# One load of 128 rows, split into a transfer of 80 rows and one of 48 rows in four pieces

## The chip, the cores and the metric

The kernel runs on one core of a Trainium2 chip. The metric is the device time of one execution in microseconds (us), the median of several runs. Profiles come from one execution taken with the hardware profiler on. The core has a matrix engine (PE), a vector engine (DVE), a scalar engine (ACT), GpSimd (POOL) and a sync engine (SP), each with an instruction queue of its own, and 16 DMA engines that carry what the queues issue.

## The reference

`x` is 128 samples of 128 channels by 1024 times in float32 (512 KB a sample, 64 MB in all). Each sample has a subject number from 0 to 7, and there are eight 128 x 128 weight matrices. Every sample gets its subject's matrix applied to its channels, and the result is added to the sample:

```python
w = weights[subjects]                      # (128, 128, 128)
out = jnp.einsum('bct,bcd->bdt', x, w)
return x + out
```

64 MB are read and 64 MB written, whatever the order.

## The kernel before

Four samples (`G * H`, with `G = 2` and `H = 2`) make a slot's content; there are 32 such groups (`NT`), called i, and 12 slots in SBUF (`xs`), so group i uses slot i % 12. Half a group, two samples, is a pair; pairs are the steps of the computation (64 of them, called j). A sample's number within its group is q.

All work is in one critical section whose order is written out by hand. Each engine runs its own list and meets the others at semaphores.

- ACT only issues loads. The first (L161) brings all eight weight matrices into `w_all`. Then come 128 loads, one a sample, through `load` (L121) and `transfer` (L50). A load reads the sample's 128 rows of 4 KB as 32 pieces of 16 KB (four consecutive rows each, `ROWS = 4`) and writes 128 partitions of 4 KB. From group 12 on ACT waits (L167) until the store of the group that held the slot before has landed.
- POOL copies, for each sample, the matrix of its subject out of `w_all` into one of four buffers `ws` (L196). The first copy of a pair waits for the pair's two loads (L200, semaphore `s_pair`), the second follows and signals `s_copied` (L201).
- PE multiplies (L206): two matmuls of 512 columns a sample, four a pair, into one of two PSUM buffers `ps`.
- DVE adds the products to the samples in place (L217), one addition a pair.
- SP issues the stores (`store`, L130), one of 2 MB for a whole group after its second pair; the first and the last group go in smaller stores. The last sample's store (L231) ends the program, together with ACT's waits for the stores of the last 12 groups (L228 to L230).

A transfer adds 16 to its semaphore once all of it has landed. The load of the pair's two samples therefore brings `s_pair` to 32 above what the slot's earlier use left (`loaded`, L116; `emptied`, L111).

Of the kernel before, what the change touches and what calls it, by code (L numbers as in the profile page):

```python
# [30 lines left out]
G = 2  # L31
H = 2
# [3 lines left out]
SLOTS = 12  # L36
# [5 lines left out]
DMA = 16  # L42

IDLE = 3

ROWS = 4
QUEUES = {mybir.EngineType.SP: "qSPDynamicHW", mybir.EngineType.Activation: "qActDynamicHW"}


def transfer(nc, engine, out, in_):  # L50

    later, nc._always_lower_symbolic_ap = nc._always_lower_symbolic_ap, False
    ins, outs = engine.lower_ap_dma(in_), engine.lower_ap_dma(out)
    nc._always_lower_symbolic_ap = later
    return engine.add_instruction(  # L57
        mybir.InstDMACopy(
            name=nc.get_next_instruction_name(),
            engine=engine.engine,  # L60
            ins=ins,
            outs=outs,
            mode="Copy",
            cce_op=ALU.bypass,
            queue=QUEUES[engine.engine],
        )
    )


@with_exitstack  # L70
def kernel(
    ctx: ExitStack,
    tc: tile.TileContext,
    x: bass.AP,
    subjects: bass.AP,
    weights: bass.AP,
    out: bass.AP,
):
    nc = tc.nc
    B, C, T = x.shape  # L80
    S, _, D = weights.shape
    NT = B // (G * H)

    def sbuf(name, *shape, dtype=F32):
        return ctx.enter_context(nc.sbuf_tensor(name, list(shape), dtype)).ap()

    given, near, wrap, index = (
        sbuf(name, 1, B, dtype=I32) for name in ("given", "near", "wrap", "index")
    )
    w_all = sbuf("w_all", C, S, D)  # L90
    ws = [sbuf(f"w{i}", C, 1, D) for i in range(W_SLOTS)]
    zeros = sbuf("zeros", C, N)
    xs = [sbuf(f"x{i}", C, H * G, T) for i in range(SLOTS)]
    ps = [
        ctx.enter_context(nc.psum_tensor(f"ps{i}", [D, G, T], F32)).ap() for i in range(P_SLOTS)
    ]

    s_given = tc.alloc_semaphore("s_given")
    s_wall = tc.alloc_semaphore("s_wall")
    s_index = tc.alloc_semaphore("s_index")  # L100
    s_zeros = tc.alloc_semaphore("s_zeros")
    s_copied = tc.alloc_semaphore("s_copied")
    s_product = tc.alloc_semaphore("s_product")
    s_added = tc.alloc_semaphore("s_added")

    s_pair = [[tc.alloc_semaphore(f"s_pair{i}_{h}") for h in range(H)] for i in range(SLOTS)]


    s_first = tc.alloc_semaphore("s_first")

    def emptied(i, h):  # L111

        turns = i // SLOTS
        return (DMA * G + (DMA if h == H - 1 else 0)) * turns

    def loaded(i, q):  # L116

        h = q // G
        return s_pair[i % SLOTS][h], emptied(i, h) + DMA * G

    def load(engine, i, q):  # L121
        k, h = i % SLOTS, q // G
        transfer(
            nc,
            engine,
            xs[k][:, q, :],
            x[i * H * G + q].rearrange("(a r) t -> a (r t)", r=ROWS),
        ).then_inc(s_pair[k][h], DMA)

    def store(i, q0, q1):  # L130
        k, b = i % SLOTS, i * H * G
        transfer(
            nc,
            nc.sync,
            out[b + q0 : b + q1].rearrange("g d t -> d g t"),
            xs[k][:, q0:q1, :].rearrange("d (o g) t -> d o (g t)", g=min(G, q1 - q0)),
        ).then_inc(s_first if i == 0 and q1 == G else s_pair[k][(q1 - 1) // G], DMA)

    with tc.tile_critical():  # L139

        nc.sync.dma_start(given, subjects.rearrange("(o b) -> o b", o=1)).then_inc(s_given, DMA)

        nc.vector.memset(zeros, 0.0).then_inc(s_zeros, 1)  # L143
        nc.tensor.wait_ge(s_zeros, 1)
        for _ in range(IDLE):
            nc.tensor.matmul(  # L146
                ps[P_SLOTS - 1][:, G - 1, :N], zeros[:, :D], zeros, start=True, stop=True
            )

        nc.vector.wait_ge(s_given, DMA)
        nc.vector.tensor_scalar(near, given, -S, S - 1, ALU.max, ALU.min).then_inc(s_index, 1)  # L153
        nc.vector.wait_ge(s_index, 1)
        nc.vector.tensor_scalar(wrap, near, 0, S, ALU.is_lt, ALU.mult).then_inc(s_index, 1)  # L155
        nc.vector.wait_ge(s_index, 2)
        nc.vector.tensor_tensor(index, near, wrap, ALU.add).then_inc(s_index, 1)  # L157
        nc.gpsimd.wait_ge(s_index, 3)


        nc.scalar.dma_start(w_all, weights.rearrange("s c d -> c s d")).then_inc(s_wall, DMA)  # L161
        for i in range(NT):
            k = i % SLOTS
            if i == SLOTS:
                nc.scalar.wait_ge(s_first, DMA)
            if i >= SLOTS:
                nc.scalar.wait_ge(s_pair[k][H - 1], emptied(i, H - 1))  # L167
            for q in range(H * G):
                load(nc.scalar, i, q)


        for j in range(NT * H):
            i, q0, q1 = j // H, j % H * G, (j % H + 1) * G
            k = i % SLOTS
            p = ps[j % P_SLOTS]

            ahead = j < P_SLOTS
            if ahead:  # L180
                nc.tensor.wait_ge(*loaded(i, q0))
            for q in range(q0, q1):
                b = i * H * G + q
                if b % R == 0:
                    _, subject = nc.values_load_multi_w_load_instructions(
                        index[0:1, b : b + R],
                        engines=[mybir.EngineType.Pool],
                        min_val=0,
                        max_val=S - 1,
                        skip_runtime_bounds_check_because="the index is clamped on the chip above",  # L190
                    )
                if b == 0:
                    nc.gpsimd.wait_ge(s_wall, DMA)
                if not ahead and q == q0:
                    nc.gpsimd.wait_ge(s_added, j - P_SLOTS + 1)
                copy = nc.gpsimd.tensor_copy(  # L196
                    ws[b % W_SLOTS], w_all[:, bass.ds(subject[b % R], 1), :]
                )
                if not ahead and q == q0:
                    copy.wait_op(*loaded(i, q0), "sem-ge")  # L200
            copy.then_inc(s_copied, 1)  # L201

            nc.tensor.wait_ge(s_copied, j + 1)
            for q in range(q0, q1):
                for t in range(0, T, N):
                    mm = nc.tensor.matmul(  # L206
                        p[:, q % G, t : t + N],
                        ws[(i * H * G + q) % W_SLOTS][:, 0, :],
                        xs[k][:, q, t : t + N],
                        start=True,  # L210
                        stop=True,
                    )
            mm.then_inc(s_product, 1)

            mine = xs[k][:, q0:q1, :]
            nc.vector.wait_ge(s_product, j + 1)
            nc.vector.tensor_tensor(  # L217
                mine, p, mine, ALU.add
            ).then_inc(s_added, 1)

            if i == 0 or q1 == H * G or i == NT - 1:
                nc.sync.wait_ge(s_added, j + 1)
                store(i, q0 if i in (0, NT - 1) else 0, q1 - (b == B - 1))

    with tc.tile_critical() as waits:
        for i in range(NT - SLOTS, NT):  # L228
            nc.scalar.wait_ge(s_pair[i % SLOTS][H - 1], emptied(i + SLOTS, H - 1))
        nc.scalar.wait_ge(s_pair[(NT - 1) % SLOTS][0], emptied(NT - 1 + SLOTS, 0) + DMA)  # L230
    last = nc.sync.dma_start(out[B - 1], xs[(NT - 1) % SLOTS][:, H * G - 1, :])  # L231

    tc.add_manual_dep(
        last.ins,
        waits.name,
        mybir.DependencyInfo(mybir.DependencyClass.NoSync, mybir.DependencyReason.SCHED_ONLY),
        reason="the end of the program waits for it",
    )
# [27 lines left out]
```

## Time and profile before

| What | Value |
|---|---|
| time, median of 3 runs | 325.85 us (325.69 to 325.96) |
| time of the profiled run | 326.15 us |
| its span, first to last instruction | 324.4 us |
| PE busy | 240.2 us (74%) |
| DVE busy | 147.9 us (46%) |
| POOL busy | 34.3 us (11%) |
| HBM read, written | 67.63 MB, 67.11 MB |
| issue of a load on ACT's queue, shortest, median, longest | 478, 1255, 4269 ns |
| SP's last wait, for the stores | 18.8 us |

The span is what the trace shows of the program; the run's time has 1.75 us more around it. An engine's busy share is a mean over the whole span and says nothing of who waits for whom; that is read from the idle time before a group of instructions and from what ended it. DMA figures are means over the 16 DMA engines. The page has the load queue as q10 (issued by ACT), the store queue as q1 (issued by SP) and instruction packets, with which the engines' programs are brought in, as q8 and q14.

### The profile page before, as it was taken

To read this page: it belongs to the slowest core of one execution; us is meant where nothing else is said; L and a number is where in the kernel's file an instruction comes from. 1 tells how busy PE (TensorE), PEld (TensorE's weight loads), DVE (VectorE), ACT (ScalarE), POOL (GpSimd) and SP (SyncE) were. 2 spreads that over 40 slices of the span, in tenths; PEclk is the share of its full clock that TensorE was granted. 3 is DMA by queue.
4 is the path that set the end of the run, shared out by engine and by line. 5 is a ranking of instruction groups with operands and counts; after the bars stand their busy time and mean duration, and the time that the engine had idled before them with its cause. 6 is when DMAs were issued, how large, how long until landed. Compare 5 with 4: busy or idle time off the path is not lost.

```text
span 324.4 us, 1608 instructions
## 1 busy us (share of the span) xinstructions
PE 240.2 (74%) x518; PEld 94.5 (29%) x518; DVE 147.9 (46%) x68; POOL 34.3 (11%) x132
## 2 busy tenths in 40 slices
PE   7999987888888888888988888888888768000000
PEld 2444432333333333333333333333333323000000
DVE  1475754555555555555555555554554553200000
POOL 1011110111111111111011111111111010000000
PEclk9999999999999999999999999999999999855555
DMA  7999999999999999999999999999999999999995
GB/s 263 402 418 426 426 421 425 425 425 423 428 425 422 427 418 427 427 424 424 428 423 421 423 427 426 419 429 426 423 426 427 417 435 417 425 427 424 429 426 243
DMA packets 16074, 134.85 MB, mean 416 GB/s; under 512 B 2625, under 2 KB 3650, under 8 KB 3906
## 3 DMA queue, kind: packets, MB, share of 16 engines
q10 hardware_dynamic: 7184, 67.64, 49.8%
q1 hardware_dynamic: 8882, 67.11, 49.3%
q8 instruction: 4, 0.07, 0.1%
q14 instruction: 4, 0.03, 0.0%
HBM read 67.63 MB, written 67.11 MB: 415 GB/s over the span
## 4 chain that ended last, share of the span: by engine, by line
PE 41%; DVE 20%; issue 18%; POOL 4%; DMA 2%; POOLq 1%; ACTq 0%; SPq 0%
PE ps L206 41%; DVE x L217 20%; POOL w L196 4%; DMA x<-in_x_dram 2%; POOLq L196 1%; ACTq L57 0%; ACTq L161 0%; ACTq L262 0%; SPq L139 0%
## 5 line engine op out<-in xcount | busy, mean ns | idle before, releaser
L206 PE MATMUL ps<-x,w 128*128 128x512 f32 x512 | 234.7, 604 | 33.6 <-POOL w L196 32.9
L217 DVE TENSOR_TENSOR x<-ps,x 128x2048 f32<-128x2048 f32 x64 | 146.7, 2292 | 128.1 <-PE ps L206 128.1
L206 PEld LDWEIGHTS ps<-x,w 128*128 128x128 f32 x512 | 92.6, 189 | 176.5 <-issue 92.3
L196 POOL COPY w<-w_all 128x128 f32 x128 | 34.1, 296 | 237.2 <-DMA x<-in_x_dram 207.2
L146 PE MATMUL ps<-zeros 128*128 128x512 f32 x6 | 5.5, 1088 | 1.7 <-DVE zeros L143 1.7
L146 PEld LDWEIGHTS ps<-zeros 128*128 128x128 f32 x6 | 1.8, 328 | 3.7 <-issue 2.1
L143 DVE MEMSET zeros<- 128x512 f32 x1 | 0.5, 485 | 1.1 <-SPq L139 1.1
L153 DVE TENSOR_SCALAR near<-given 1x128 int32<-1x128 int32 x1 | 0.2, 216 | 0.6 <-DMA given<-in_itok_B_dram 0.6
L157 DVE CUSTOM_DVE_ANT_0 index<-near,wrap 1x256 uint16<-1x256 uint16 x1 | 0.3, 278 | 0.0
L155 DVE TENSOR_SCALAR wrap<-near 1x128 int32<-1x128 int32 x1 | 0.2, 215 | 0.0
L253 POOL MEMSET const-float32-0.0<- 128x1 f32 x1 | 0.1, 99 | 0.2 <-issue 0.2
L253 POOL MEMSET const-bfloat16-1.0<- 128x1 bf16 x1 | 0.1, 102 | 0.0
L253 POOL MEMSET const-uint8-127<- 128x1 uint8 x1 | 0.1, 102 | 0.0
L253 POOL MEMSET const-float32-1.0<- 128x1 f32 x1 | 0.1, 99 | 0.0
## 6 DMA issues: line engine op xcount, KB each, us to landing
x<-in_x_dram ACTq DMA_DIRECT2D x128, 512.0 KB, 32.2
out_dram<-x SPq DMA_DIRECT2D x30, 2048.0 KB, 46.9
out_dram<-x SPq DMA_DIRECT2D x3, 1024.0 KB, 13.8
out_dram<-x SPq DMA_DIRECT2D x2, 512.0 KB, 21.0
w_all<-in_L_cond_weights_dram ACTq DMA_DIRECT2D x1, 512.0 KB, 4.3
given<-in_itok_B_dram SPq DMA_DIRECT2D x1, 0.5 KB
```

The source lines that it names most:

```text
L143: nc.vector.memset(zeros, 0.0).then_inc(s_zeros, 1)
L146: nc.tensor.matmul(ps[P_SLOTS - 1][:, G - 1, :N], zeros[:, :D], zeros, start=True, stop=True)
L153: nc.vector.tensor_scalar(near, given, -S, S - 1, ALU.max, ALU.min).then_inc(s_index, 1)
L155: nc.vector.tensor_scalar(wrap, near, 0, S, ALU.is_lt, ALU.mult).then_inc(s_index, 1)
L157: nc.vector.tensor_tensor(index, near, wrap, ALU.add).then_inc(s_index, 1)
L196: copy = nc.gpsimd.tensor_copy(ws[b % W_SLOTS], w_all[:, bass.ds(subject[b % R], 1), :])
L206: mm = nc.tensor.matmul(p[:, q % G, t : t + N], ws[(i * H * G + q) % W_SLOTS][:, 0, :], xs[k][:, q, t : t + N], start=True, stop=True,)
L217: nc.vector.tensor_tensor(mine, p, mine, ALU.add).then_inc(s_added, 1)
L253: nc = _bacc.Bacc("TRN2", target_bir_lowering=False, num_devices=1)
```

## The change

The load of sample q = 1 of group i = 8 (in slot 8, the 34th of the 128 loads) is issued as two transfers. The first moves rows 0 to 79, row by row, into partitions 0 to 79 and signals the pair's semaphore as the whole load did. The second moves rows 80 to 127 as four pieces of 12 rows (48 KB each) into partitions 80 to 127 and signals a semaphore of its own, `s_uneven`. POOL waits for that semaphore before it copies this sample's matrix. The bytes moved are the same, and all other loads, the stores and the computation are as they were.

```diff
+UNEVEN = (8, 1)
+EVEN, FEW = 80, 4
...
+    s_uneven = tc.alloc_semaphore("s_uneven")
...
+    def load_uneven(engine, i, q):
+        k, h, b = i % SLOTS, q // G, i * H * G + q
+        transfer(nc, engine, xs[k][:EVEN, q, :], x[b, :EVEN, :]).then_inc(
+            s_pair[k][h], DMA
+        )
+        rest = x[b, EVEN:, :].rearrange("(a r) t -> a (r t)", a=FEW)
+        transfer(nc, engine, xs[k][EVEN:, q, :], rest).then_inc(s_uneven, DMA)
...
             for q in range(H * G):
-                load(nc.scalar, i, q)
+                (load_uneven if (i, q) == UNEVEN else load)(nc.scalar, i, q)
...
                 if b == 0:
                     nc.gpsimd.wait_ge(s_wall, DMA)
+                if (i, q) == UNEVEN:
+                    nc.gpsimd.wait_ge(s_uneven, DMA)
```

## The prediction

> **What bounds the kernel now.** I read the page first: slices, DMA queues, then the groups.
>
> ```profile
> span 324.4 us, 1608 instructions
> ...
> DMA  7999999999999999999999999999999999999995
> GB/s 263 402 418 426 426 421 425 425 425 423 428 425 422 427 418 427 427 424 424 428 423 421 423 427 426 419 429 426 423 426 427 417 435 417 425 427 424 429 426 243
> DMA packets 16074, 134.85 MB, mean 416 GB/s; under 512 B 2625, under 2 KB 3650, under 8 KB 3906
> ...
> q10 hardware_dynamic: 7184, 67.64, 49.8%
> q1 hardware_dynamic: 8882, 67.11, 49.3%
> q8 instruction: 4, 0.07, 0.1%
> ...
> L196 POOL COPY w<-w_all 128x128 f32 x128 | 34.1, 296 | 237.2 <-DMA x<-in_x_dram 207.2
> ```
>
> The 16 DMA engines are full from the second slice to the last but one, and the two data queues take 99.1% of all their time. POOL, at the head of the computation, is idle 237.2 us, 207.2 of them waiting for loads. So bytes set the time, not PE (74%) or DVE (46%). How far ahead the queues are stands in the DMA issues:
>
> ```profile
> x<-in_x_dram ACTq DMA_DIRECT2D x128, 512.0 KB, 32.2
> out_dram<-x SPq DMA_DIRECT2D x30, 2048.0 KB, 46.9
> ```
>
> A load lands 32 us after its issue, a store 47 us after: each engine always has both kinds waiting. The last DVE addition begins at 275.5 us; the rest drains stores. The end therefore belongs to whichever DMA engine has its work done last, so the third view is a row of windows over the last microseconds:
>
> ```profile
> 319.00:320.00 1.00, 0.00 (x0) 0.00 (x0) 0.00 (x0) 0.00 (x0) 0.50 1.02 418
> 320.00:320.50 0.50, 0.00 (x0) 0.00 (x0) 0.00 (x0) 0.00 (x0) 0.50 0.84 344
> 320.50:321.00 0.50, 0.00 (x0) 0.00 (x0) 0.00 (x0) 0.00 (x0) 0.50 0.53 213
> 321.00:321.50 0.50, 0.00 (x0) 0.00 (x0) 0.00 (x0) 0.00 (x0) 0.50 0.36 147
> 321.50:322.00 0.50, 0.00 (x0) 0.00 (x0) 0.00 (x0) 0.00 (x0) 0.50 0.22 90
> 322.00:322.50 0.50, 0.00 (x0) 0.00 (x0) 0.00 (x0) 0.00 (x0) 0.50 0.10 41
> 322.50:323.00 0.50, 0.00 (x0) 0.00 (x0) 0.00 (x0) 0.00 (x0) 0.50 0.04 16
> 323.00:324.40 1.40, 0.00 (x0) 0.00 (x0) 0.00 (x0) 0.00 (x0) 0.50 0.00 0
> ```
>
> The last two columns are the DMA share and GB/s. Share times 16 is the number of engines at work: 16, 13.4, 8.5, 5.8, 3.5, 1.6, 0.6, none. The engines do not finish together. The shares after 320 sum to 2.09; times 0.5 us that is 1.05 us, a mean end of 321.05 us, while the last engine works to about 322.95. No balancing can bring more than these 1.9 us (0.6%).
>
> Which engine is late, and why, I worked out from the trace's single packets. They carry start, duration, size and queue but no engine. On one engine the next packet starts 3 or 4 ns before the last one's recorded end, and each engine gets the same order of packets (two of 16 KB and one of 4 B for every load, 16 of 8 KB and one of 4 B for most stores), so they string together into 16 chains that use every packet. Two chains that end a packet within a few ns of each other may be exchanged; the ends are not affected. The chains' last packets start at (us)
>
> 320.12 320.30 320.30 320.44 320.51 320.69 320.72 320.76 320.90 321.10 321.23 | 321.73 321.79 322.01 322.24 322.95
>
> Eleven are early, five late. Four of the late ones each carried one of the four 16 KB instruction packets (q8) that come at 47.6, 115.8, 182.8 and 250.7 us, take 974 to 1098 ns and put their chain some 1.5 us behind. The latest has none; it loses 2.1 us little by little between 20 and 280 us (its 8 KB packets take 316 ns, the others' 311).
>
> **The change, part by part.** *Bytes per engine.* Loads are now given in 32 pieces of 16 KB, and the records show 4096 packets of 16 KB: a piece is one packet, two per engine and load. The index load, one piece, is one packet of 512 B and one of 4 B: one engine. So four pieces go to four engines, and 80 rows to all 16 with five each. An 8 KB packet occupies its engine for 307.5 ns (311 less the overlap), a 16 KB one 613, a 4 KB one (only the last two stores have them) 155.5, a 4-byte one 6.
>
> - Twelve engines: 2 x 613 = 1226 becomes 5 x 155.5 = 777.5, so 0.45 us less.
> - Four engines: 777.5 + 6 + 3 x 613 = 2622.5, so 1.40 us more. A 48 KB packet is not in this trace. Below, three load packets at their quickest (611 recorded) give the same 1.40. Above, three times the instruction packet's mean 1.04 us give 3.1 us instead of 1.84, so 2.7 us more. I take 1.40: the load row is the same kind of transfer.
>
> A rule of the Trainium skill speaks against this part: DMA: Bandwidth & Descriptors, in its Rules for kernel authors, says an outermost dimension of fewer than 16 keeps a transfer to that many engines and should be avoided. By it alone the piece of 48 rows is a loss of 1.4 us where those engines end last; that is the second rival's sum, and no row here shows such a transfer.
>
> *One more issue on ACT's queue.* An issue of a load takes 478 to 4269 ns, median 1255. The 94 loads behind it come that much later; the cover is the 32.2 us from issue to landing. Cost nothing; 1.3 us without the cover, and nothing to gain.
>
> *One more wait on POOL*, for the uneven part, before the second weight copy of pair 16. Behind it wait that copy, PE's products of the pair, DVE's addition, and then the store of slot 8. The four engines are late by 1.40 us of work; as loads take half of an engine's time (49.8% against 49.3%), by up to 2.8 us of landing. The cover is the store backlog (46.9 us) and the loads queued meanwhile: no engine runs dry. Cost nothing; 1.4 to 2.8 us if the stores had no backlog. The first copy's wait counts the same as before.
>
> *Sum.* An engine that ends at E now ends at E - 0.45 or E + 1.40. If the four are all among the early eleven, the end is 322.95 - 0.45 = 322.50, or at most 321.23 + 1.40 = 322.63: 0.32 to 0.45 us earlier. The profiled run took 326.15 us, 1.75 more than its span; the median of the timed runs is 325.85, 0.30 less. I set the difference against the median: 325.40 to 325.53, say 325.45, a gain of 0.12%. A measurement here can tell about 0.2% (0.65 us) from no change, so this counts as none.
>
> Which four, the trace does not say. From both ends: -0.45, and +1.40 if the latest is one of them. I take the value of the typical engine (the median end is 320.83 and becomes 322.23, still ahead of 322.50). By lots all four are early in 330 of 1820 draws, 0.18. But four pieces of one transfer will hardly be scattered, and the instruction packets, evenly spaced and each on another engine, look as if handed out in turn. Two runs of four neighbours in a ring of 16 miss each other in 9 of 16 cases; times 0.8 for the latest one, 0.45.
>
> **The rivals.**
>
> - *An instruction-packet engine is among the four.* For it: four of 16 are such. Against: the trace names none. It ends at 321.73, 321.79, 322.01 or 322.24 plus 1.40 = 323.13 to 323.64, 0.18 to 0.69 later: 326.03 to 326.54, mostly still within 0.2%.
> - *Slower: the slowest engine is among the four.* Its place is the final drain: 322.95 + 1.40 = 324.35, so 327.25. Any engine that now ends after 322.95 - 1.40 = 321.55 and is given a piece turns the gain into a loss; this one decides alone. For it: 4 in 16 by lots. Against: four engines carry the instruction packets and are not it. The Trainium skill (the same page, Latency and other measured facts) names engines 7 and 15 as usually slower, and (Why a DMA increments its semaphore by 16 and not by 1) has a small transfer use the lowest-numbered engines; by that this rival falls. The trace has one slow engine but no numbers.
> - *The four pieces are spread over all 16 engines*, so that nothing is shifted: 16 engines with 777.5 + 6 + 12 KB (460) = 1243.5 against 1226, no change: 325.85. Against: the one-piece index load.
> - *Faster: the slow engine's drift depends on how its loads and stores alternate*, and the load at 65 to 68 us shifts that. By then 0.7 of its 2.1 us are lost; if the other 1.4 fall away, the end is 322.24 - 0.45 = 321.79, so 324.7. For it: no drift in the pure stores after 280 us. Against: it holds steadily through 250 us of changing phases.
>
> **How the numbers follow.** Forecast 0.45, instruction engine 0.28, slowest engine 0.16, not shifted 0.04, faster 0.07. The likeliest alone would range from 325.2 to 325.7. With the second and third cases it has to reach 327.4 (327.25 and the spread of runs, 0.15); the drift case stays out below: 325.0 to 327.4. Faster by over 0.2% (below 325.20): 0.07 and the forecast's edge, 0.12. Slower (above 326.50): 0.16, the last of the instruction engines (0.07) and a 48 KB packet at its upper bound (0.04), 0.27. Within: 0.61.
>
> **What would show it.** In the profile after, packets of q10 rise by 52 data packets (80 + 4 - 32) and 4 more of 4 B. In the windows of the end, twelve engines stop 0.45 us earlier and four 1.4 later; the last engine stops at 322.5. An end at 324.3 with one engine alone for over a microsecond means the slowest engine got a piece; at 323.1 to 323.7, an instruction engine. If the DMA share dips below 0.9 between 60 and 280 us, the covers were wrong, and so is the sum.

## The result

The changed kernel takes 327.35 us (median of 6 runs, 326.94 to 327.69), the kernel before 325.77 (6 runs, 325.52 to 326.41). The ratio is 1.0043, 95% interval [1.0033, 1.0053]: 1.6 us slower, where no measurable change was forecast. The profiled run of the changed kernel took 326.94 us; it is the quickest of the six, so its trace shows a smaller loss than the medians do. Its page:

```profile
span 325.2 us, 1609 instructions
...
DMA  7999999999999999999999999999999999999995
GB/s 252 419 407 426 423 427 421 421 408 426 424 425 426 425 424 423 420 428 427 423 430 420 422 425 421 431 425 419 430 421 426 421 423 427 425 428 423 429 425 232
DMA packets 16130, 134.85 MB, mean 415 GB/s; under 512 B 2629, under 2 KB 3654, under 8 KB 3990
...
q10 hardware_dynamic: 7240, 67.64, 49.8%
q1 hardware_dynamic: 8882, 67.11, 49.2%
```

The load queue has 56 packets more, 52 of data and 4 of 4 bytes, as foreseen: four pieces of 48 KB, 80 rows of 4 KB. The DMA engines stay full, and the bytes are the same. The windows of the end, again with the DMA share and GB/s in the last two columns:

```profile
320.00:320.50 0.50, 0.00 (x0) 0.00 (x0) 0.00 (x0) 0.00 (x0) 0.50 0.88 360
320.50:321.00 0.50, 0.00 (x0) 0.00 (x0) 0.00 (x0) 0.00 (x0) 0.50 0.74 303
321.00:321.50 0.50, 0.00 (x0) 0.00 (x0) 0.00 (x0) 0.00 (x0) 0.50 0.56 229
321.50:322.00 0.50, 0.00 (x0) 0.00 (x0) 0.00 (x0) 0.00 (x0) 0.50 0.42 172
322.00:322.50 0.50, 0.00 (x0) 0.00 (x0) 0.00 (x0) 0.00 (x0) 0.50 0.30 123
322.50:323.00 0.50, 0.00 (x0) 0.00 (x0) 0.00 (x0) 0.00 (x0) 0.50 0.20 82
323.00:323.50 0.50, 0.00 (x0) 0.00 (x0) 0.00 (x0) 0.00 (x0) 0.50 0.08 33
323.50:324.00 0.50, 0.00 (x0) 0.00 (x0) 0.00 (x0) 0.00 (x0) 0.50 0.02 8
```

Between 322.0 and 323.0, where 1.6 and 0.6 engines were still at work before (shares 0.10 and 0.04), it is now 4.8 and 3.2. The last engine stops at 323.74 instead of 322.95, and the span is longer by as much (0.8 us). Strung together into 16 chains as before, one for each engine, the packets give these ends (us); a star marks a chain that carries a 48 KB packet:

320.10 320.27 320.34 320.52 320.76 320.86 321.15 321.56 321.74 321.81* 322.10 322.34 322.71 323.03* 323.17* 323.74*

The engine that drifts (8 KB packets of 315 ns against 311 to 313) is the one at 322.34. It carries no large piece. So the four are early engines, as forecast, and yet three of them are now last. Three theories remained:

- A: the four engines set the end, by their bytes, by pieces that take longer than the 1.84 us assumed, and because they were not as early as assumed.
- B: the slowest engine is one of the four (the rival of the prediction, whose 327.25 us fits the time well); then the chains would be wrong.
- C: the split itself costs, through the extra issue, POOL's wait, or pairs that come late. Its variant D, a rival in two later runs: the loss is paid once, at the place where the split load stands.

### The profile page after: what moved, and what is told of

Read it like the earlier page. It is cut to its first block, busy times and chain, and to the rows that moved or that the text cites. A ratio compares the mean times of both kernels' runs of the same rounds, so it can differ in the third digit from the quotient of the medians.

```text
span 325.2 us, 1609 instructions
## 1 busy us (share of the span) xinstructions
PE 241.3 (74%) x518; PEld 95.2 (29%) x518; DVE 147.8 (45%) x68; POOL 34.1 (10%) x132
## 4 chain that ended last, share of the span: by engine, by line
PE 29%; DVE 17%; issue 14%; ACTq 11%; DMA 10%; POOL 3%; POOLq 1%; SPq 0%
PE ps L222 29%; DVE x L233 17%; ACTq L61 11%; DMA x<-in_x_dram 10%; POOL w L212 3%; POOLq L212 1%; POOLq L199 0%; ACTq L175 0%; ACTq L278 0%; SPq L153 0%
```

## The experiments

Each kernel changes the changed kernel. Times are medians beside runs of the kernel before on the same chip.

**all16: split and wait kept, no uneven engines.**

```diff
-        rest = x[b, EVEN:, :].rearrange("(a r) t -> a (r t)", a=FEW)
-        transfer(nc, engine, xs[k][EVEN:, q, :], rest).then_inc(s_uneven, DMA)
+        transfer(nc, engine, xs[k][EVEN:, q, :], x[b, EVEN:, :]).then_inc(s_uneven, DMA)
```

> The load of sample (8, 1) is still split into 80 and 48 rows, with the second semaphore and POOL's wait, but the 48 rows go row by row to all 16 engines. Theory A (the end is set by the four engines that got the big pieces; they were early ones, but the piece took longer than 1.84 us and they started late): every engine has 8 rows again, 1250 ns instead of 1226, so 325.8 us. Theory B (the slowest engine of before is one of the four): also 325.8. Theory C (the split, its extra issue or POOL's wait costs the time): 327.3, as in the changed kernel.

Measured 325.99 us, ratio 1.0003 [0.9994, 1.0012]. The split, its issue and the wait cost nothing that can be measured; C falls. Pairs that come late only because a large piece is late are left to double and at24.

**three16: the same bytes on the four, in 16 KB pieces.**

```diff
-        rest = x[b, EVEN:, :].rearrange("(a r) t -> a (r t)", a=FEW)
-        transfer(nc, engine, xs[k][EVEN:, q, :], rest).then_inc(s_uneven, DMA)
+        for r0 in range(EVEN, 128, 16):
+            rest = x[b, r0 : r0 + 16, :].rearrange("(a r) t -> a (r t)", a=FEW)
+            transfer(nc, engine, xs[k][r0 : r0 + 16, q, :], rest).then_inc(s_uneven, DMA)
```

(POOL waits for all three.)

> The 48 rows go to four engines as before, but as three transfers of four 16 KB pieces instead of one of four 48 KB pieces. The four engines' bytes are the same. Theory A: if the 48 KB packet's excess over 1.84 us (0.03 to 0.63 us in the changed kernel's trace) comes from its size, 326.9 us; if it comes from four engines writing the upper partitions, 327.3. Theory B: 327.3 whichever, and the slowest engine carries three 16 KB pieces. Theory C: 327.3 or, with two more issues, up to 328.

Measured 326.76 us, 1.0024 [1.0014, 1.0033]. Two more issues, and yet not slower than the changed kernel; by the medians 0.6 us less, though the intervals just touch. The two traces don't show this difference (profiled runs 326.92 and 326.94). In this one, too, the four with pieces are among the last five: 322.47, 322.82, 322.87 and 323.70.

The trace also shows that it does not take large packets to lengthen packets. Windows from 66 to 72 us, DMA share and GB/s in the last two columns, first of all16:

```profile
66.00:72.00 6.00, 4.12 (x9) 1.44 (x8) 4.00 (x2) 0.79 (x3) 1.00 1.03 430
```

and of three16:

```profile
66.00:72.00 6.00, 3.07 (x8) 1.04 (x6) 3.38 (x2) 0.29 (x1) 1.00 1.03 410
```

three16 has no packet above 16 KB, and yet its engines, equally full, move 410 GB/s; the changed kernel has 408 here and the kernel before 426 (lines below). Of its 16 KB load packets between 64 and 76 us, 32 take over 630 ns, up to 798; in all16 none does.

**marker: which engine is which.** 64 rows go to all 16 engines, and the rest in eight, four and two pieces, so that the number of pieces on a chain tells its group.

```diff
-EVEN, FEW = 80, 4
+EVEN = 64
...
+        for r0, r1, few in ((64, 96, 8), (96, 112, 4), (112, 128, 2)):
+            rest = x[b, r0:r1, :].rearrange("(a r) t -> a (r t)", a=few)
+            transfer(nc, engine, xs[k][r0:r1, q, :], rest).then_inc(s_uneven, DMA)
```

(POOL waits for all three again.)

> The load of sample (8, 1) is dealt so that its packets tell which engine a chain is: 64 rows to 16 engines (4 each), 32 rows in eight pieces of 16 KB, 16 rows in four of 16 KB, 16 rows in two of 32 KB. Two engines get 20 rows (+1.87 us of work against 8 rows), two 12 (+0.63), four 8 (+0.02), eight 4 (-0.60). Theory A: the two with 20 rows end last, 0.5 us later than the four of the changed kernel at most, so 327.3 to 327.8; the slowly drifting engine and those with 16 KB instruction packets have no 32 KB and none of the four-piece packets. Theory B: the drifting engine has them; 327.8 if it is one of the two, 326.5 if one of the next two. Theory C: three more issues and waits, 327.3 to 329.

Measured 327.15 us, 1.0039 [1.0024, 1.0053]. The chains, read from the packets:

| Engines | Rows | Ends (us), and instruction packets they carry (time) |
|---|---|---|
| pieces of all three transfers | 20 | 323.23; 323.58 (8 KB at 109) |
| of the first two | 12 | 322.43 (8 KB at 177); 323.39 (8 KB at 62 and 196) |
| of the first only | 8 | 320.90; 320.93; 322.36 (16 KB at 186); 323.30, the drifting one |
| of none | 4 | 320.52; 320.75; 320.76; 321.12; 321.22; 321.85, 322.06, 322.52 (16 KB at 47, 119, 253) |

The groups are nested: whoever has a piece of the transfer in two has one of those in four and in eight. That agrees with the Trainium skill's rule (DMA: Bandwidth & Descriptors, Why a DMA increments its semaphore by 16 and not by 1) that a transfer dealt to fewer than 16 engines takes the lowest-numbered ones. The drifting engine is in the third group, the fifth to eighth; engine 7, which the same page of the Trainium skill (Latency and other measured facts) calls usually slower, would be in it, though the page's guess at the reason concerns transfers whose descriptors software makes, and the queues here are listed as hardware_dynamic. B falls. (In eight64 and eightmid, below, the 16 KB instruction packet of 253 us is on an engine with a piece, so two chains of the last two rows may be exchanged here; nothing below rests on them.) And three of the four that a four-piece transfer uses carry all the 8 KB instruction packets.

**even112: fewer bytes on the four.** `EVEN, FEW = 112, 4`.

> The same split with 112 rows over 16 engines and 16 rows in four pieces of 16 KB (4 rows each): the four get +0.48 us of work, the twelve -0.14. Theory A: the four (early, ends up to 321.9 before) come to 322.4, the drifting engine to 322.8: 325.7 to 325.9. Theory B: 322.95 + 0.48, so 326.3. Theory C: 327.3, as the wait and the issue are the same.

Measured 325.82 us, 0.9998 [0.9989, 1.0007]: as A has it. B's 326.3 (a ratio of 1.0015) lies outside, and this does not rest on the chains.

**double: two such loads.** `UNEVEN = ((8, 1), (9, 1))`, with a semaphore for each.

> Sample (9, 1) is loaded in the same two parts as (8, 1). Theory A (the four engines end last, by their bytes and by the longer packets): they end 1.40 us later again, up to 2.0 with the second set of 48 KB packets, so 328.8 to 329.4 us. Rival D (the changed kernel's loss is paid once, in the stretch around 67 us, for instance by delayed pairs): 327.4 to 327.8.

Measured 329.26 us, 1.0101 [1.0084, 1.0119]: a second such load costs 0.58% more, 1.9 us, so the loss is not paid once. Its windows show the four without any chains:

```profile
322.00:322.50 0.50, 0.00 (x0) 0.00 (x0) 0.00 (x0) 0.00 (x0) 0.50 0.36 147
322.50:323.00 0.50, 0.00 (x0) 0.00 (x0) 0.00 (x0) 0.00 (x0) 0.50 0.24 98
323.00:323.50 0.50, 0.00 (x0) 0.00 (x0) 0.00 (x0) 0.00 (x0) 0.50 0.24 98
323.50:324.00 0.50, 0.00 (x0) 0.00 (x0) 0.00 (x0) 0.00 (x0) 0.50 0.24 98
324.00:324.50 0.50, 0.00 (x0) 0.00 (x0) 0.00 (x0) 0.00 (x0) 0.50 0.24 98
324.50:325.00 0.50, 0.00 (x0) 0.00 (x0) 0.00 (x0) 0.00 (x0) 0.50 0.28 115
325.00:325.50 0.50, 0.00 (x0) 0.00 (x0) 0.00 (x0) 0.00 (x0) 0.50 0.16 66
325.50:326.00 0.50, 0.00 (x0) 0.00 (x0) 0.00 (x0) 0.00 (x0) 0.50 0.10 41
```

A share of 0.24 to 0.28 is four engines of 16: for over two microseconds the other twelve have nothing left and four still drain. A loss from late pairs would hold up all sixteen, not these four.

**at24: another place.** `UNEVEN = (24, 1)`.

> Only the place is changed: the split load is sample (24, 1), the 98th, instead of (8, 1). Theory A: bytes per engine are the same and the place does not matter: 327.3 us. Rival D: another place has another price; with loads of this slot already waiting for its store, more than 327.6.

Measured 327.21 us, 1.0029 [1.0018, 1.0040], which overlaps the changed kernel's. No effect of the place is shown, and with double, D falls. In this trace (span 325.6 us) the four carry pieces of 2278 to 2713 ns and end at 322.38, 323.51, 323.69 and 324.14, the latest of the others at 322.50.

**low48: the four write other partitions.** Rows 0 to 47 in pieces, 48 to 127 row by row.

```diff
-EVEN, FEW = 80, 4
+LOW, FEW = 48, 4
...
+        transfer(nc, engine, xs[k][LOW:, q, :], x[b, LOW:, :]).then_inc(
...
+        rest = x[b, :LOW, :].rearrange("(a r) t -> a (r t)", a=FEW)
+        transfer(nc, engine, xs[k][:LOW, q, :], rest).then_inc(s_uneven, DMA)
```

> Rows 0 to 47 go in four pieces, rows 48 to 127 row by row; partitions 0 to 47 instead of 80 to 127 are written by the four. Theory A as to the end: 327.3 us. If the 48 KB packets' excess (1871 to 2467 ns instead of 1839) hangs on the partitions they write, it changes: 326.8 without it. If it hangs on four engines reading or writing large pieces at once: 327.3, and the ordinary 16 KB packets beside them again take up to 800 ns.

Measured 326.68 us, 1.0015 [1.0006, 1.0024], with pieces of 2100, 2106, 2264 and 2540 ns. The time came out as it would without the excess, but the packets have the excess all the same (mean 2253 ns, the changed kernel's 2230). What differs is beside them: 14 ordinary 16 KB loads take over 630 ns, to 794, against 20, to 811. The intervals of the two kernels lie apart, 0.28% between the ratios, but the traces hardly differ (326.85 and 326.94 us; the last engine ends at 323.67 and 323.74). So theory A's 327.3 did not come, the pieces do not explain why, and it stays open.

**eight64 and eightmid: eight pieces of 32 KB**, rows 64 to 127 in the one (`EVEN, FEW = 64, 8`) and rows 32 to 95 in the other, whose edit is:

```diff
-EVEN, FEW = 80, 4
+LOW, HIGH, FEW = 32, 96, 8
...
+        transfer(nc, engine, xs[k][:LOW, q, :], x[b, :LOW, :]).then_inc(
...
+        transfer(nc, engine, xs[k][HIGH:, q, :], x[b, HIGH:, :]).then_inc(s_uneven, DMA)
+        rest = x[b, LOW:HIGH, :].rearrange("(a r) t -> a (r t)", a=FEW)
+        transfer(nc, engine, xs[k][LOW:HIGH, q, :], rest).then_inc(s_uneven, DMA)
```

> 64 rows over 16 engines (4 each) and 64 rows in eight pieces of 8 rows (32 KB): engines one to eight get 12 rows (+0.63 us against 8), the other eight 4 (-0.60). Theory A with the marker's reading (the drifting engine is one of the fifth to eighth, the four first carry the 8 KB instruction packets): the drifting engine ends at 322.95 + 0.63 = 323.58, up to 0.3 more for a longer packet: 326.5 to 326.8 us. If the marker was misread and the drifting engine is one of the last eight: 322.35 for it and 322.6 at most for the others, 325.6.

> As eight64 (eight pieces of 8 rows, 32 KB), but the pieces are rows 32 to 95 instead of 64 to 127; rows 0 to 31 and 96 to 127 go to all 16 engines in two transfers of two rows each. Bytes per engine are the same as in eight64, so by bytes alone the time is 326.5 to 326.8 us there and here. Theory E (the excess of the large packets comes from the partitions that several engines write at once, eight64's all in the upper half): the 32 KB packets fall from 1791 to 2351 ns towards 1226 to 1600, and the time from 328.05 to 326.5 or 327.0. Rival F (the excess comes from eight large pieces at once, wherever they are written): 1800 to 2300 ns and 328.0 us again.

Measured 328.05 us, 1.0057 [1.0042, 1.0072], and 327.26 us, 1.0040 [1.0026, 1.0053]. In eight64 the drifting engine carries a piece and ends last at 325.39, as the marker had it; by bytes alone it would have been 323.58. Its piece took 2271 ns instead of the 1226 of two 16 KB packets, which is 1.05 of these 1.81 us. All eight took 1791 to 2351 (mean 2107) there, and in eightmid 1226 to 1889 (mean 1722), the 1226 by the one that began 0.7 us ahead of the rest. So place has a part (E), but 1.7 us is still far from 1.23, and pieces that run at once last longer in both places (F). The windows from 66 to 72 us, last columns share and GB/s, first of the kernel before:

```profile
66.00:72.00 6.00, 5.69 (x13) 2.47 (x14) 3.99 (x2) 0.53 (x2) 1.00 1.01 426
```

of the changed kernel:

```profile
66.00:72.00 6.00, 3.23 (x8) 1.14 (x6) 3.54 (x2) 0.59 (x2) 1.00 1.03 408
```

of eight64:

```profile
66.00:72.00 6.00, 3.70 (x8) 1.44 (x8) 3.99 (x2) 0.49 (x2) 1.00 1.03 346
```

and of eightmid:

```profile
66.00:72.00 6.00, 3.90 (x9) 1.57 (x10) 3.85 (x2) 0.59 (x2) 1.00 1.02 386
```

The engines are full in all four (1.01 to 1.03) while what they move falls from 426 to 408, 346 and 386 GB/s: packets last longer, engines do not wait for work. What lengthens them was not tried further; by three16's 410 GB/s it is not the packet size alone.

## Why the prediction was wrong

- *What bounds the kernel* was right: all16, even112 and double move the end as the bytes of the last engines do.
- *One more issue, one more wait* were rightly put at nothing. POOL's copies of the kernel before, from its timeline:

```profile
69.42 0.53 POOL L196 COPY w<-w_all 128x128 f32 x2 [3.48 <-DMA x<-in_x_dram]
73.73 0.53 POOL L196 COPY w<-w_all 128x128 f32 x2 [3.77 <-DMA x<-in_x_dram]
```

and of the changed kernel:

```profile
69.40 0.29 POOL L212 COPY w<-w_all 128x128 f32 x1 [3.93 <-DMA x<-in_x_dram]
71.71 0.29 POOL L212 COPY w<-w_all 128x128 f32 x1 [2.01 <-DMA x<-in_x_dram]
75.91 0.53 POOL L212 COPY w<-w_all 128x128 f32 x2 [3.91 <-DMA x<-in_x_dram]
```

  The second copy of pair 16 waits 2.0 us for the uneven part, and the next pair comes 2.2 us later than before: within the 1.4 to 2.8 us foreseen. The DMA engines had other work meanwhile: their share is 1.03 from 66 to 72 us, and every slice of the page but the first and the last has a 9.
- *Which four* was right as far as the forecast went: "all among the early eleven". They are the carriers of the 8 KB instruction packets and one more. The first rival, one of the late carriers of the 16 KB instruction packets among the four, did not happen: no starred chain carries one.
- *The step that failed* is the bound that followed: the end is 322.50 "or at most 321.23 + 1.40 = 322.63". Both of its terms were too small. The term of 1.40 us holds a piece of three 16 KB packets, 1.84 us; the four pieces took 1.87, 2.26, 2.33 and 2.47, so 1.43 to 2.03 us in all. (The bound of 2.7 from above was in the text and was given a chance of 0.04.)
- *The other term of that bound*, 321.23, is the latest early engine of one trace and no bound in another run. The last engine now, at 323.74, would have ended at 323.74 - 2.03 = 321.71. It carries the 8 KB packet of 177 us, and the engine that carried that one before (at 174 us) ended at 321.10. As far as the chains can be told apart, most of this difference of 0.61 us stands already in the first loads: from the second to the sixth, up to 12 us, the engine is 0.33 to 0.55 us behind the median engine, where its counterpart was 0.10 ahead. Such a start differs from trace to trace (at the sixth load of all16 from 0.5 us ahead to 0.7 behind). No chains are needed to see that the engines came to the split load at different times: the four pieces begin at 66.96, 67.81, 68.09 and 68.29 us, in the order of their sizes above. From 322.63: plus 0.63 for the piece, and plus 0.48 because this engine would have ended at 321.71 and not by 321.23, is 323.74.
- *The twelve's gain* of 0.45 us was mostly lost too. By the forecast's terms the mean end of the sixteen stays (twelve times 0.45 less, four times 1.40 more); it rose from 321.05 to 321.60 us (shares after 320 sum to 3.20, times 0.5 us). Counted by the bytes moved so far, the changed kernel is 0.14 us behind at 65 us, 0.50 at 75 us, and 0.53 at 315 us: most is lost in the ten microseconds of the split load. There, 20 ordinary loads took 638 to 811 ns instead of 616, 2.1 us together, and the pieces' excess is 1.6; over 16 engines that is 0.23 of the 0.36 us. The same ten microseconds cost 0.36 us in three16, without a large packet, and 0.03 in all16. So the forecast also put at nothing what a load dealt to four engines does to the other packets.
- *The size of the loss.* The two traces account for 0.8 us (326.94 against 326.15 in the profiled runs). The medians differ by 1.6, since the one profiled run is the quickest of six and the other 0.4 above its median. at24's trace, whose span of 325.6 us is the middle of the changed kernel's, has pieces up to 2713 ns and the last engine at 324.14, 0.4 later; the longer piece (2713 ns against 2467) is 0.25 of that. The changed kernel's own slower runs have no trace here, so the other 0.8 us is not taken apart, and neither is why low48 loses less.
- *The rival that gave 327.25 us*, the slowest engine among the four, came within 0.1 us of the time and is wrong: marker and even112 exclude it.

None of these versions is measurably faster than the kernel before. In the traces a transfer in four or eight pieces always went to the same engines, and they include all that carry the 8 KB instruction packets, and for eight the drifting one.

## What to carry to other kernels

Where all DMA engines are full, as here, the end belongs to the engine that has its work done last, so look at how the DMA share falls in the last microseconds before shifting bytes; count what each engine carries besides the data. An end read from one trace is no bound: leave it the spread of its start. A transfer dealt to a few engines cost more here than its bytes: its own packets and its neighbours' lasted longer. And a rival that hits the time still has to be asked for its mechanism.

## What the runs showed that was not expected

- Instruction packets keep to their engines. The 8 KB ones (four within the span) lie on three of the four lowest engines, two of them on the same one, in every trace where the pieces tell the engines apart but even112, where two chains may be exchanged. The 16 KB ones lie on other engines.
- While a load is dealt to a few engines, load packets last longer: in the runs with eight pieces, 32 KB take 1226 ns for one that is ahead of the others and 1691 to 2351 for those that run together, and ordinary 16 KB loads beside them up to 1095 ns instead of 616. The rate of all 16 engines falls to 346 GB/s with every engine busy. Pieces of 16 KB are enough: three16 falls to 410 GB/s.
- One engine, of the fifth to eighth, takes 314 to 317 ns for its 8 KB packets, the others 311 to 313, through most of each run and loses about 2 us to the others.
